# One vision-transformer layer on one core: the orders of all five engines written out, PSUM and exponential tiles in turn

## The chip, the core and the metric

The kernel runs on one core of one Trainium2 chip. The time is device microseconds of one execution. The core's engines each have their own instruction queue and run it in order: TensorE (PE: matrix products, with weight loads PEld), VectorE (DVE), ScalarE (ACT: functions such as sine and exponential), GpSimd (POOL), and SyncE (SP), which here issues nearly all DMA transfers. Engines wait for each other by semaphores. SBUF is the on-chip memory, PSUM the small memory into which TensorE writes.

## What is computed

Sixteen images of 3 x 512 x 512 are cut into 1024 patches of 768 values each and pass through one layer of width 256:

```python
h = patches @ W.T + b                                  # 16 x 1024 x 256
# attention, 8 heads of 32
q, k, v = split(layernorm(h) @ w_qkv)
k = sum_f kan_a[f]*sin(f*k) + kan_b[f]*cos(f*k)        # f = 1 .. 256, elementwise
attn = softmax(q @ k.T / sqrt(32))
h = h + (attn @ v) @ w_out + b_out
# feed forward: a shared network and the best 2 of 4 experts
x = layernorm(h)
h = h + shared(x) + sum over 2 experts of weight * expert(x)
```

All is in float32.

## The kernel before, in words

The 256 sines and cosines of every key element are made from sums of two angles: "slow" waves `w` and "fast" waves `f`. The keys' angles lie in DRAM (`ud`). For a *group* of eight rows of keys, DMA brings two tiles `w` of 128 x 1024 from `ud` (line 995), with each row repeated over many partitions; a third tile `f` is spread by a VectorE shuffle (line 1035, letter D below) from a source tile `src` that serves eight groups (line 1014). GpSimd multiplies each tile by its frequencies (L1050, T). ScalarE takes the sine (L1060, F). TensorE mixes the two `w` into a PSUM tile `kan` (L1080, M), VectorE multiplies that by `f` (L1094, P), TensorE adds up two such products (L1113, R). After eight groups the keys of one pair of heads are ready; VectorE splits them in a high and a low part (K) and they go through DRAM into their place.

Attention takes one pair of heads and half of the queries at a time. For each of eight key blocks, TensorE writes a score tile `sT` (L1179, S), ScalarE its exponential `es` (L1194, also F), TensorE adds it, weighed by values and by ones, into `av` (L1212, W). VectorE divides (N).

A *round* is four groups of waves (twelve sines) and eight scores and exponentials. ScalarE first does a round's exponentials and then the sines of another; a table load stands at each change (at L1332, behind the sines, a dummy exponential `few` forces it). An image has eight rounds.

All else is in four *chains*: generators that yield, step by step, on which engine their next step runs. Chain 0 makes keys, queries and values; chain 1 the output projection and the networks; chain 2 the experts' weights; chain 3 the tokens and the first layernorm. In an order a chain's step stands as the digit of the chain. Two steps matter below. `transposed_layernorm` lets GpSimd find the scale, ScalarE normalize four blocks `hn` (L546), TensorE transpose them in two groups `lnT` (L334) and ScalarE copy each into `hT` (L555). `gates` then multiplies `hT` by the gate weights (`gate`, L816): its first four products need the first copy, its last four the second.

Scores and `kan` share two PSUM buffers of 1024 columns, pool `big`: a score or a `kan` waits until the exponential or the product two tiles before it is done. Chain steps use two other PSUM buffers, `side`. The waves `w` have eight buffers, the `f` four, the exponentials five. TensorE works in three tilings: whole (scores, transposes), four columns of 32 (`av`, `red`, the gate) and eight tiles of 64 x 32 (`kan`); a chain step can be done whole (line 325) or in columns (line 328), and `tiling_of` picks the one that suits its neighbours.

The program is straight-line code, and Python lays it out: a planner holds a modelled clock for every engine. TensorE's order is a string, `ORDER`: for each token the planner lays that step on TensorE. Before it, `others` lays whatever on the other four engines can begin by then, the earliest first. So the other engines' orders, and SyncE's DMA issues, come from the planner's costs and due times. `begin` gives a step's earliest time from what it depends on; `put` queues the steps; `lay` and `lay_at` emit one. The eleven middle images repeat one piece of the string.

Of the kernel before, what the change touches and what calls it, by code (L numbers as in the profile page):

```python
# [11 lines left out]
FP = mybir.dt.float32  # L12
# [55 lines left out]
ORDER = (  # L68
    "33333331311003033003000M0M00M0M0MRR330M",
    "33R3M3MRM330M3R3MM0SRSSWSWSSWSSWWW0MWM3",  # L70
    "WRMMSSSRSSWWSSWSW0WWWM3MWMMRSSRSSWSWSSWSWWWW0WMMM0MRSSRSSWSSWSWSWWWWWMM0MMRSSSWSWSSWSSWW"
    "WRMWMWMRMSSSWSSWSWSSWRWWWW0M0M0MM0SSSRSSRWWWS3SW3SWWWW3MM31RMM1SSRWSWSSWSWSSWWWW3MM3MS10"
    "SRSWMWSSWW3SWSSR31WWW0MMMRMS0SS1WSS1WSW1R1SSWWW01MMWW1RM10SS1SMWSS1SSW1SWW1R01MMWWWWR1MM"
    "1SSR1SSW1SSWWSS1W1MMWWWMWMRS0S1SR1SSW1WW1SS1SWW01WWMM1WRM3SS1SSWWM1SSW1SS3R1WWWW1MWMM31S"
    "SRWM0SS1SS0SSWW0W3RW1WM01MM1SSWRWSS1SMW3SSWWR3SWWW1WWMM3RMM1SS0SSWWSS1SSW13WWRMM3WWWM31S"
    "SR1SSWMW1W1SS3RW3SS1WWWW10M1MM1RMS1SS0SSWWSSW1SRW01WWMM1SWW0RM10SS1SM1WR1SSWWSS1WW1WWWMM"
    "3SSRMMWS1SW1SS0SSWW0W1R3WMMWWM31SS1SSWRMW1WSS1SSW1WRW1WW10",
    (
        "MM1MM1RSS10SS1SSW1WW1SSW0RWWWWMM1RMM3SS0SSWWWSS1SS3RWW1WWW3MM10MM3SRRWSS1SSWS1SSWW3WWWMM"
        "3W31S1RM1MWS13SSR3SS1SSWW0WWW1WMMW1RMM1S0SS1SSW1SS0SWWWR1WWWW01MM10MM1SSR1WSSRWW1SS0SS1W"  # L80
        "WWWWMM1S0SRWSSWWMMW1SS3SS1WWWR13WMM31MM1RSS1SSWWWSS1SSRWWW1WW101"
    )
    * 11,
    "MM1MMR0SS1SS0SSWWW1SSW1RW3W1MM10MM1SSWW",
    "RSS1SS3RWW3SSWWW1WWW3MM1MMRS0SS1SSWS1SSWWRWWWWW3M31MM3SS1RM1SWWSSR1W3SSW3SW01WWWM1M0M1RM"
    "S1SS1SSWRWSSW1S01WWW1MM1WW0MM1SSR1SSWR1SSWWSS1WW0WWMMW1SS0SRSSWMWWS1SW1SMWWR10W1MMW1MM1R"
    "SS1SSW1SS1SSWWWRW1W1WW10MM10MM1SSR1SSWWSSW1SSRWW1MMWWWRMM1SS0SSWWSSWSSRWWW1MWW10M1RSS1SS"
    "WSSWSMWSMWWWWRMM1W1R1M1M1SS1SSWWSS1SSWW1RW1WW1WM1M1MS1RS1SSW1SSW1SSWMWWWRWMM1SWS1SRSSWMM"
    "WS1SW1SRW1WW1M1MW1WR1MS1SSWSWSS1SSWWWM1WR1MMWW1RM1M1SSRWSSW1SSWW1SSWWWWSS1SSWWSSWWSSWWWW"
    "S1SW1SS1SSWWSSWWWWW11110110111101000101010100010001000100",  # L90
# [3 lines left out]
def plain_path(ctx: ExitStack, tc: tile.TileContext, a: dict, out: bass.AP, verdict: bass.AP):  # L94
# [29 lines left out]
    esp = pool("esp", NES)  # L124
# [4 lines left out]
    big = pool("big", 2, PSUM)  # L129
# [151 lines left out]
    lanes = [0.0] * 8  # L281

# [142 lines left out]
    def lay(engine, queue):  # L425
        cost, deps, key, action = queues[engine][queue].pop(0)
        at = begin(engine, deps)
        clock[engine] = at + cost
        done[key] = clock[engine] + TAIL[engine]
        action()  # L430

    def heads(engine):
        for rank, (name, steps) in enumerate(queues[engine].items()):
            at = begin(engine, steps[0][1]) if steps else None
            if at is not None:
                yield at, rank, name

    def others(limit):

        soonest = None  # L440
        again = True
        while again:
            again = False
            soonest = None
            for engine in (SP, POOL, ACT, DVE):
                while True:
                    settle()
                    best = min(heads(engine), default=None)
                    chain = min(wanting(engine), default=None)
                    if chain and (  # L450
                        best is None
                        or chain[0] < best[0]
                        or (chain[0] == best[0] and best[2] not in ("prod", "keys"))
                    ):
                        at, lay_it = chain[0], lambda c=chain[1]: step(c)
                    elif best:
                        at, lay_it = best[0], lambda q=best[2]: lay(engine, q)
                    else:
                        break
                    if at > limit:  # L460
                        soonest = at if soonest is None else min(at, soonest)
                        break
                    lay_it()
                    again = True
        return soonest

    def lay_fixed(kind):

        cost, deps, key, action = queues[PE][kind][0]
        at = begin(PE, deps + (bigs[-2:-1] if kind in USERS else []))  # L470
        return at, lambda: lay_at(kind, at)

    def lay_at(kind, at):

        cost, deps, key, action = queues[PE][kind].pop(0)
        if kind == "S" and now["tiling"] is not None:
            cost += RELOAD
        clock[PE] = at + cost + retile(TILINGS.get(KINDS[kind]), at > clock[PE] + 0.03)
        done[key] = clock[PE] + TAIL[PE]
        user = USERS.get(kind)  # L480
        if user:
            bigs.append((user, *key[1:]))
        action()

    def run():

        order = "".join(ORDER)
        for i, token in enumerate(order):
            now["ahead"] = order[i + 1 : i + 4]
            while True:  # L490
# [1596 lines left out]
```

## Time and profile before

| what | value |
|---|---|
| runs shown | 3893.35, 3896.15, 3896.16 us; median 3896.15 |
| profiled execution, its run | 3898.54 us |
| profiled execution, its span | 3896.9 us |
| granted TensorE clock, mean | 0.994 |
| moved by DMA | 916.54 MB, 235 GB/s |
| sines (L1060), waves `w` and `f` | 1024 and 512, mean 1048 and 1046 ns |
| exponentials (L1194) | 1024, mean 1023 ns |
| GpSimd turns (L1050) | 1536, mean 1895 ns |
| shuffles (L1035) | 512, mean 1371 ns |
| products (L1094) | 512, mean 1215 ns |
| table loads | 128 at L1060, 128 at L1332, mean 1283 ns |

The profile is of one execution. "Busy" is the time in which an engine had an instruction in work; TensorE's ends are modelled and its instructions overlap, so its starts say more than its ends. A time line gives the start, the length, the engine, the line, the operation, its tiles as out<-in, the count, and in brackets the idle time before it with what ended that. Several instructions of a kind can stand in one row.

### The profile page before, as it was taken

The numbers are of one execution on the slowest core, as the hardware profiler recorded it, in microseconds if no ns is written. First come the engines' busy times: TensorE is split into PE (matmuls) and PEld (weight loads), VectorE is DVE, ScalarE is ACT, GpSimd is POOL, SyncE is SP. The second block draws the span as 40 slices with busy tenths as digits, with TensorE's granted clock in tenths as the row PEclk, the third lists the DMA queues.
The fourth block names the chain that finished last, engine by engine and source line by source line (L and its number), as shares of the span: only waits on it lengthen the run. The fifth ranks groups of instructions, "written<-read, shape, count | busy, mean of one in ns | idle before, by whom it ended". The sixth has DMA issues, their size and how long they took to land.

```text
span 3896.9 us, 103136 instructions
## 1 busy us (share of the span) xinstructions
PE 3791.3 (97%) x40457; PEld 1942.1 (50%) x40457; DVE 2544.1 (65%) x4075; ACT 3256.0 (84%) x3939; POOL 3193.6 (82%) x2328
## 2 busy tenths in 40 slices
PE   7899999999999999999999999999999999999998
PEld 4334454555545555455454545545455554544444
DVE  4657757666675766757666675776767667576652
ACT  2698888888888888888888888888888888889983
POOL 3899878888888878879788888878879888898860
PEclk9999999999999999999999999999999999999999
DMA  7898978878887887878888788788878888878760
GB/s 229 259 276 231 274 213 239 257 230 250 229 260 223 248 257 227 264 218 259 245 239 251 217 251 243 232 250 243 256 215 253 250 234 258 226 236 250 219 177 18
DMA packets 589665, 916.54 MB, mean 235 GB/s; under 512 B 60876, under 2 KB 179572, under 8 KB 589172
## 3 DMA queue, kind: packets, MB, share of 16 engines
q1 hardware_dynamic: 588036, 909.40, 79.6%
q8 instruction: 322, 5.28, 0.6%
q14 instruction: 171, 1.40, 0.1%
q10 hardware_dynamic: 1136, 0.47, 0.0%
HBM read 758.64 MB, written 150.99 MB: 233 GB/s over the span
## 4 chain that ended last, share of the span: by engine, by line
PE 77%; ACT 10%; DMA 7%; DVE 2%; issue 2%; POOL 1%; SPq 1%; ACTq 0%; POOLq 0%; DVEq 0%
PE av L1212 19%; PE sT L1179 11%; PE kan L1080 9%; PE red L1113 5%; PE tok L325 4%; ACT w L1060 4%; DMA w<-ud 3%; PE e1p L325 3%; PE tok L328 3%; PE e3p L325 3%; PE e1p L328 2%; ACT f L1060 2%; PE k L325 2%; PE proj L325 2%; PE s1p L325 1%
## 5 line engine op out<-in xcount | busy, mean ns | idle before, releaser
L1050 POOL TENSOR_TENSOR w<-w,lane 128x1024 int32<-128x1024 int32 x1024 | 1924.4, 1895 | 356.9 <-DMA w<-ud 252.2
L1194 ACT ACTIVATE es<-sT 128x1024 f32<-128x1024 f32 x1024 | 1004.0, 1023 | 369.0 <-PE sT L1179 305.9
L1060 ACT ACTIVATE w<-w 128x1024 f32<-128x1024 int32 x1024 | 1013.3, 1048 | 48.8 <-POOL w L1050 40.6
L1050 POOL TENSOR_TENSOR f<-f,lane 128x1024 int32<-128x1024 int32 x512 | 970.4, 1895 | 101.0 <-DVE f L1035 96.7
L1094 DVE TENSOR_TENSOR f<-kan,f 128x1024 f32<-128x1024 f32 x512 | 605.5, 1215 | 228.9 <-ACT f L1060 120.2
L1179 PE MATMUL sT<-q,k 128*128 128x512 f32 x2048 | 689.1, 450 | 14.0 <-DVE f L1094 7.8
L1035 DVE STREAM_SHUFFLE f<-src 128x1024 int32<-128x1024 int32 x512 | 681.1, 1371 | 1.0
L1212 PE MATMUL av<-es,v 128*32 128x256 f32 x8192 | 638.1, 383 | 11.1 <-ACT es L1194 11.1
L1212 PE MATMUL av<-es,ones 128*32 128x256 f32 x8192 | 630.5, 379 | 0.0
L1080 PE MATMUL kan<-w,coef 64*32 64x512 f32 x8192 | 529.3, 598 | 15.3 <-ACT w L1060 9.6
L1060 ACT ACTIVATE f<-f 128x1024 f32<-128x1024 int32 x512 | 514.2, 1046 | 13.1 <-POOL f L1050 13.1
L1179 PEld LDWEIGHTS sT<-q,k 128*128 128x128 f32 x2048 | 360.7, 189 | 254.0 <-issue 110.7
L1212 PEld LDWEIGHTS av<-es,v 128*32 128x32 f32 x8192 | 233.1, 109 | 347.9 <-issue 219.4
L1212 PEld LDWEIGHTS av<-es,ones 128*32 128x32 f32 x8192 | 266.5, 110 | 176.4 <-issue 0.9
L1236 DVE RECIPROCAL rc<-av 128x256 f32<-128x256 f32 x128 | 224.7, 1756 | 161.7 <-PE av L1212 161.6
L1080 PEld LDWEIGHTS kan<-w,coef 64*32 64x32 f32 x8192 | 123.9, 105 | 311.4 <-issue 144.7
L1113 PE MATMUL red<-f,pack 128*32 128x512 f32 x2048 | 269.8, 599 | 1.6 <-DVE f L1094 1.6
L325 PE MATMUL tok<-wt,x 128*128 128x256 f32 x780 | 186.9, 391 | 14.8 <-DMA x<-in_xT 11.2
L325 PEld LDWEIGHTS tok<-wt,x 128*128 128x128 f32 x780 | 147.4, 194 | 70.5 <-issue 29.2
L1060 ACT ACT_TABLE_LOAD x128 | 164.2, 1283 | 21.9 <-DMA w<-ud 19.7
L328 PE MATMUL tok<-wt,x 128*32 128x256 f32 x3024 | 176.3, 381 | 2.5 <-DVE ui L637 2.0
L1332 ACT ACT_TABLE_LOAD x128 | 164.2, 1283 | 2.2
(150 smaller groups left out, 4252.1 us busy)
## 6 DMA issues: line engine op xcount, KB each, us to landing
w<-ud SPq DMA_DIRECT2D x2048, 256.0 KB
q<-qd SPq DMA_DIRECT2D x512, 128.0 KB
k<-kd SPq DMA_DIRECT2D x256, 256.0 KB
x<-in_xT SPq DMA_DIRECT2D x128, 384.0 KB
ud<-u SPq DMA_DIRECT2D x64, 512.0 KB
ud<-ui SPq DMA_DIRECT2D x64, 512.0 KB
src<-ud SPq DMA_DIRECT2D x512, 64.0 KB
qd<-qhi SPq DMA_DIRECT2D x64, 256.0 KB
```

What stands on the lines that cost most here:

```text
L325: nc.tensor.matmul(out=out, lhsT=lhsT, rhs=rhs, start=start, stop=stop)
L328: nc.tensor.matmul(out=out[ts(i, 32)], lhsT=lhsT[:, ts(i, 32)], rhs=rhs, start=start, stop=stop)
L1035: nc.vector.stream_shuffle(w, sources[g // 8].rearrange("p r n -> p (r n)"), [4 * (g % 8) + i // 8 for i in range(32)],)
L1050: nc.gpsimd.tensor_tensor(w, w, f.to_broadcast([P, N]), ALU.mult)
L1060: nc.scalar.activation(x, w, AF.Sin, scale=TURN * 2.0**-32)
L1080: nc.tensor.matmul(out=ps[ds(64 * j + 32 * blk, 32), ts(r, 512)], lhsT=coef[ts(r, 64)].rearrange("p e f j -> p (e f j)"), rhs=w[ts(r, 64), ...
L1094: nc.vector.tensor_mul(w, kan.pop(g), w)
L1113: nc.tensor.matmul(out=rows_of_pair[p][ts(2 * i + r, 32), :], lhsT=pack[:, ds(PACK0 - 16 * (k % 2) - 2 * (k // 2), 32)], rhs=prod[:, ts(r, ...
L1179: nc.tensor.matmul(out=ps[:, ts(s, 512)], lhsT=k4[kc // 4][:, s, ts(kc % 4, P)], rhs=q4[:, s, :], start=True, stop=True,)
L1194: nc.scalar.activation(es, scores.pop(kc), AF.Exp, scale=SCALE)
L1212: nc.tensor.matmul(out=acc[0][ts(i, HD), ts(half, 256)], lhsT=ones32 if half else v[:, kc, p % NPAIR, ts(i % 2, HD)], rhs=es[:, ds(512 * ( ...
L1236: nc.vector.reciprocal(rc[0], acc[0][:, 256:512])
```

## The change

Instead of one order for TensorE there are five, one for each engine, all written out (`ORDERS`: a list of parts, each with its number of repeats and the orders of TensorE, ScalarE, VectorE, GpSimd and SyncE). The four loops that chose the other engines' steps are gone. `run` now looks at the next token of each engine, takes the one that can begin first by the planner's clock, and emits it; what is decided is only how the five fixed orders are woven into one program. A chain step that ends in a DMA says so (`SENDS`), and is emitted only when SyncE's order has come to the same chain's digit.

```diff
-ORDER = (
...
-        "MM1MM1RSS10SS1SSW1WW1SSW0RWWWWMM1RMM3SS0SSWWWSS1SS3RWW1WWW3MM10MM3SRRWSS1SSWS1SSWW3WWWMM"
-        "3W31S1RM1MWS13SSR3SS1SSWW0WWW1WMMW1RMM1S0SS1SSW1SS0SWWWR1WWWW01MM10MM1SSR1WSSRWW1SS0SS1W"
-        "WWWWMM1S0SRWSSWWMMW1SS3SS1WWWR13WMM31MM1RSS1SSWWWSS1SSRWWW1WW101"
-    )
-    * 11,
...
+STEPS = {
+    PE: {"M": "M", "R": "R", "S": "S", "W": "W"},
+    ACT: {"F": "fixed"},
+    DVE: {"P": "prod", "K": "keys", "N": "norm", "D": "spread"},
+    POOL: {"T": "turn"},
+    SP: {"A": "source", "W": "waves", "X": "tokens", "K": "keys", "Q": "queries"},
+}
+SENDS, SENT_KEYS = "sends", "S"
+ORDERS = (
...
+    (
+        11,
+        "MM1MMR1RSS10SS1SSW1WW1SSW0WWWWMM1RMM3SS0SSWWRSS1SS3WWWWWW1MM310MM1SSRRSS1SSWWSSW3W3WMMWW"
+        "3W31SSR1SSW1MMW1S3SWR3SSWW10W1WMMW1RMM1S0S1SSWWR1SS0SSWW1WWWW10MM10MM1SSRWSS1WWR1SS0SS1W"
+        "WWWWMM1SSR0WSSWMMWW1SS31SSWRWWW13MM13MMR1SS1SSWWSS1SSWRW1WWWW101",
+        "F1FFF1FF10FFFF1F1F0FFFFFF0FFFFFFFFFFF0FFFF3333F3FFFFFFFF3FFFFFFFFFFFFFFFFFFF1F1F1FF1FFFF"
+        "1FF1FF331332F3F3FF2FF1FFFFF1FFFF1FFF1FF1FFF1FFF1FFFFF1FFFFFFFF1FF1FFFFFFFFFFFFFFFFFFFFFF"
+        "1111F1F1FFFFF1FFFFFFFFFF12FFF1FFF12FFF1FFFFF1F",
+        "PPPP1DDDD1NNPP1PNPND3D3333KDD1N1PNNPN10PP010D1DD11131DP3P3NN3N333N3DPP1D2DKD000P2PN2NPPN"
+        "N0D00DD0D00NN0P1PNPPND0D1DKD10NPNNP1N111D1D0PP3DDNNNN3P1PP3PD22DD2KNNDNN",
+        "TTTTTTTTTTTTTTTTT3TTTTTT0TTT3T0TTTTT1TTTTTTT3TTTT22TTTTT20TT2T3T0TTTTT0TTTTTTTTTTTTTTTTT"
+        "T1TTTTTTTTTTTTTT22T2TTTT2TT",
+        "WWWWWWAWAWAWWWAWWWXQWSQ1WKWKWWW0WWWXAWAWWAAWWWWQWWSQKWKWWWX0WW0WAWA0WXWWAA0WWW0QWSW0KWWW"
+        "1KWWXWWWQ0AAWWAWAXQWXWWXWSWKQK",
+    ),
...
-    def others(limit):
...
     def run():
 
-        order = "".join(ORDER)
-        for i, token in enumerate(order):
...
+        settle()
+        while True:
+            heads = [(head(e), i) for i, e in enumerate(clock)]
+            heads = [(at, i) for at, i in heads if at is not None]
+            if not heads:
+                break
+            at, i = min(heads)
+            lay(list(clock)[i], at)
+            settle()
```

In SyncE's orders a W is one tile of waves (two transfers), an A one quarter of a source tile (two transfers of 64 KB), X a block of patches, K and Q the keys and queries of an attention, S the transfer of finished keys, a digit a chain's. Before, the four A of a source tile stood side by side in SyncE's queue; now there are W between them.

The two PSUM buffers of `big` and the five of the exponentials, which the pool handed out, are now named one by one:

```diff
-    esp = pool("esp", NES)
+    esp = pool("esp", 1)
...
-    big = pool("big", 2, PSUM)
+    big = pool("big", 1, PSUM)
...
-            ps = kan[g] = big.tile([P, N], FP, tag="big", name="kan")
+            ps = kan[g] = big.tile([P, N], FP, tag=f"big{len(bigs) % 2}", name="kan")
...
-            es = exps[kc] = esp.tile([P, 1024], FP, tag="es", name="es")
+            es = exps[kc] = esp.tile([P, 1024], FP, tag=f"es{(att * NT + kc) % NES}", name="es")
```

The instructions of ScalarE, VectorE, GpSimd and SyncE are the same in kind and number in both programs. On TensorE some chain steps take the other of their two forms (token products in columns: 1728 instead of 1512, whole: 336 instead of 390, and smaller differences of this kind), with the same work.

## The prediction

> **What bounds the kernel now.** I read the page's engine totals first, then its stretches (busy time of each engine between given times), then the time line around the places where TensorE's records leave room. The totals and the long middle stretch:
>
> ```profile
> span 3896.9 us, 103136 instructions
> PE 3791.3 (97%) x40457; PEld 1942.1 (50%) x40457; DVE 2544.1 (65%) x4075; ACT 3256.0 (84%) x3939; POOL 3193.6 (82%) x2328
> ...
> 0.00:100.00 100.00, 70.39 (x312) 44.98 (x312) 42.09 (x80) 25.31 (x38) 40.59 (x50) 0.93 0.74 231
> 100.00:400.00 300.00, 274.95 (x3035) 116.59 (x3036) 198.43 (x298) 250.01 (x287) 273.39 (x168) 0.97 0.89 257
> ...
> 700.00:3500.00 2800.00, 2769.47 (x30159) 1448.14 (x30161) 1882.54 (x3023) 2416.03 (x2931) 2373.37 (x1718) 1.00 0.83 241
> ```
>
> The columns of a stretch are its length, then busy time (and count) of TensorE, its weight loads, VectorE, ScalarE, GpSimd, then granted clock, DMA share, GB/s. From 0.7 to 3.5 ms TensorE is busy 2769 of 2800 us at clock 1.00: it is the bound there. From 0.1 to 0.4 ms GpSimd is at 91% and ScalarE at 83%: there they feed TensorE too slowly.
>
> "Busy" overstates TensorE, since matmul ends are modelled. So I took starts: records that follow each other undisturbed start 216 ns apart (256 columns), 429 ns (512), 230 ns (scores, 512 columns in one pass), with 93 to 136 ns more where the tiling (whole, four columns of 32, eight of 64x32) changes. All instructions of the program at these rates make 3519 us, its 1297 tiling changes 145 us. First instruction at 11 us and about 10 us after the last start: some 212 us are TensorE's waits. By place, in us: 90 before 400 us, 22 from 3600 us to the end of the matmuls, 86 in the 2800 us of the middle, of which half is a fixed surcharge (score pairs after another tiling, 0.11 each). What is left to win in the middle is about 43 us.
>
> The largest part of it returns once per image, at a matmul group `kan` behind the gate matmuls:
>
> ```profile
> 1567.54 1.28 ACT L1332 ACT_TABLE_LOAD   x1
> ...
> 1568.67 0.42 PE L816 MATMUL gate<-hT,gw 128*32 128x128 f32 x8
> 1568.83 0.20 ACT L1332 ACTIVATE few<-few 128x1 f32<-128x1 f32 x1
> 1568.94 0.57 ACT L555 COPY hT<-lnT 128x512 f32<-128x512 f32 x1
> ...
> 1569.41 1.03 ACT L1194 ACTIVATE es<-sT 128x1024 f32<-128x1024 f32 x1
> ...
> 1569.56 0.43 PE L816 MATMUL gate<-hT,gw 128*32 128x128 f32 x8 [0.47 <-ACT hT L555]
> ...
> 1570.49 1.09 PE L1080 MATMUL kan<-w,coef 64*32 64x512 f32 x16 [0.50 <-ACT es L1194]
> ```
>
> Gate work is 0.44 us and its tiling change 0.11, so `kan` should start at 1568.67 + 0.55 = 1569.22; it starts at 1570.49, 1.27 late. ScalarE is the cause: copy and first exponential of the round stand behind the table switch. Worked out alike at its eleven returns from 864 to 3220 us this is 1.27 us five times and 1.96 to 2.03 six times, 18.4 us together. I call it stall A. Stall B also returns once per image, where the first `av` of a round waits for the round's first exponential, 1.22 us:
>
> ```profile
> 1418.88 1.28 ACT L1332 ACT_TABLE_LOAD   x1
> ...
> 1420.28 1.92 ACT L1194 ACTIVATE es<-sT 128x1024 f32<-128x1024 f32 x2
> ...
> 1421.34 0.64 PE L1212 MATMUL av<-es,v 128*32 128x256 f32 x8 [1.01 <-ACT es L1194]
> ```
>
> **Buffers.** Followed by address through both programs, the 1536 `big` tiles already alternate between two PSUM places, with one exception, and the 1024 exponentials take their five buffers in turn without one. Naming the buffers removes no wait: at most that one exception, under 1 us. I take 0.
>
> **Stall A in the new order.** No instruction is added or removed on ScalarE, VectorE, GpSimd or SyncE; some TensorE steps change between whole and four-column form at equal work. Before, from the eighth score S8 of a round TensorE does six `av` (0.86 each), three token blocks (2.59), two `kan` (0.86), a transpose group (0.44), a score (0.46), a transpose group, `red` (0.86), `kan`, and 0.8 of tiling changes: the gate starts 18.5 us after S8. ScalarE ends exponential 8 about 1.4 after S8 (0.37 from a score's end to its exponential, 1.03 for itself), then does a table load (1.28), twelve sines at 0.95, four `hn` (0.52), a copy (0.57), table load and dummy (1.48), the second copy (0.57), the first exponential (1.03): it ends 19.8 after S8. The `kan` behind the gate needs that exponential's PSUM buffer and could run at 19.05: late by 0.85 with the 0.1 of the release, where the trace has 1.27 to 2.0. So such a count is good to about half a microsecond.
>
> After, TensorE does a fourth token block there, then transposes, two scores, `red`, transposes, two scores, one `av`, and only then the gate: third score at 20.6, gate at 22.4, first and second `kan` behind it at 23.0 and 23.8. ScalarE's first copy goes behind the table switch, the second behind two exponentials: first exponential ends at 1.4 + 17.8 = 19.2, second 20.2, copy 20.7, third 22.4 (its score ends at 21.0), fourth 23.4. Third score, gate and both `kan` have 1.3, 1.7, 0.5 and 0.4 us in hand. Stall A goes; the least cover is 0.4 us. If ScalarE comes later than that, it returns at the excess. Eleven images: -18.4 us, bounds -18.4 and 0.
>
> I made the same count for the other seven rounds of an image. Stall B stays: 15.2 us of ScalarE against 15.6 of TensorE, both unchanged. In the remaining six the first `av` and third score have 1.2 us or more, before and after. So 0 for these, bounds +1 and -1 us an image (the rest of the middle's 43 us, less 18 of A and 13 of B, is 12), +11 and -11.
>
> A rule that speaks against this: the Trainium skill (ScalarE: Activation LUTs, "What ACT_TABLE_LOAD costs") gives a switch of table sets about 1.28 us of load and 1.38 us of drain. The trace agrees with the load, 1.28, and shows no drain: the dummy starts at 1568.83, at the end of the load. With the drain, an estimate by that page, both switches of a round would be 2.8 us longer, the first exponential would end at 22.0, the third score would wait 1.4 us and A would come back in this form: the sum would lose most of its 18. I go by the trace.
>
> **Tiling changes.** Counted in both orders: 1297 before, 1260 after, 4.6 us less at 93 to 136 ns each. 28 of the 37 fall on the first three images (-3.3 us), where GpSimd and ScalarE set the pace; ten are one per image in the middle (-1.3). The first lie partly beside waits: I take -1.0 (bounds 0 and -3.3). The last images gain and lose: 0.
>
> **Start.** Source loads (`src`) leave SyncE from 65.1 us, behind the third `ud` pair, which waits for VectorE; the first fast shuffle starts at 74.1, GpSimd's first fast turn at 75.5, and from there GpSimd is busy to 99.7. In the new order two of the four parts go ahead of that pair: about 1.5 us earlier. `kan` may start one query block sooner, but queues behind the same turns. I take -0.7 (bounds 0 and -1.5).
>
> **SyncE, GpSimd, VectorE.** The first part of each source load moves 0.91 wave loads forward, mean of 64 loads, one wave load a 1.84 us slot (29.4 us a round over 16); the last part moves 2.4 back. It waits for a shuffle whose place among VectorE's products is unchanged. Its waits now, and those behind it (wave loads, then GpSimd's turns, then sines):
>
> ```profile
> SPq L1014 <- DVE f L1035: 129.9, 48, 4.9
> ...
> POOL w L1050 <- DMA w<-ud: 252.2, 104, 6.8
> ...
> ACT w L1060 <- POOL w L1050: 40.6, 32, 9.2
> ```
>
> The columns: total wait in us, times, longest. If all 64 wait 0.91 x 1.84 longer, SyncE loses 107 us; GpSimd's 252 us of waits reach ScalarE as 41, a sixth. That would be at most 18 us, beside ScalarE's 16% of idle time. I take 0, bounds 0 and +18.
>
> **Sum.** -18.4 - 1.3 - 1.0 - 0.7 = -21.4 us. The profiled span of 3896.9 becomes 3875.5, its run 3898.5 (1.6 around the span) 3877.1. The runs shown have the median 3896.15, 2.4 under the profiled run: 3874.8, said as 3875.
>
> **Rivals.** *The wait comes back* in the same round: the new cover is 0.4 us where my count missed the old stall by 0.4 to 1.2. For it: both sides of A are ScalarE's order, and ScalarE has only moved its copies. Against it: four checks all come out with cover. It leaves the tiling and the start, -3.0: 3893.
>
> *Slower: the source loads block SyncE.* One part at the head of the queue holds the wave loads behind it. It turns the result when more than (21.4 + 7.8) of the 107 us, 27%, reach TensorE; at half it is 3896.15 - 21.4 + 53.5 = 3928. For it: 48 of 64 loads wait there already, and go forward while their shuffle doesn't. Against it: a sixth is what passes on today, and the wave loads run up to eight buffers ahead.
>
> *The order on the chip isn't what its words say*: excluded for the buffers (they already alternate), and for the rest the two programs do differ; it would be 3896.
>
> **How the numbers follow.** This kernel's runs can tell 0.2%, 7.8 us, from no change. Forecast, faster by about 21: 0.66. Wait comes back or no effect: 0.14, nearly all within 0.2%. SyncE blocks, slower: 0.20. The range goes down to 3860 (3874.8 less 2.3 and 0.8 to the bounds of tiling and start and 11 in the other rounds) and up to 3906, half-way into the slower case.
>
> **What would show it.** Right: `kan` behind the gate starts within 0.6 us of the gate in the middle images; images return every 233.7 instead of 235.5 us (from 864.6 to 3219.6 in ten steps); `av` still waits 1.2 us once per image; clock 1.00. Wrong: a third score or `kan` in that round with an idle time ended by an exponential or copy; the wait of L1014 (its new line) on the shuffle above 200 us together with ScalarE waiting over 60 us for GpSimd. Gains of more than 5 us in the first 400 us would show that I undervalued the start.

## The result, and the profile after

The changed kernel takes 3894.49 us in the median (3888.84 to 3904.53, 12 runs) beside 3896.32 of the kernel before. The ratio is 0.9994, 95% interval 0.9983 to 1.0005: no change that can be told, where 21 us of gain were forecast. (In all that follows a ratio is that of a kernel to the kernel before, measured side by side; 0.001 is 3.9 us, and an interval is about 0.001 to either side.) The profiled execution of the changed kernel has a span of 3889.6 us; its own run took 3891.19.

Behind the orders' code the lines of the new program have numbers higher by 59, those of TensorE's chain steps (L325, L328, L334) by 83: L1050, L1060, L1080, L1094, L1113, L1179, L1194, L1212, L816, L546, L555, L1014 of before are L1109, L1119, L1139, L1153, L1172, L1238, L1253, L1271, L875, L605, L614, L1073 now. (The runs below have longer order texts and other line numbers again; go by the tiles.) Totals and the stretches that were shown of before:

```profile
span 3889.6 us, 104231 instructions
PE 3789.0 (97%) x41057; PEld 1937.2 (50%) x41057; DVE 2530.3 (65%) x4075; ACT 3261.8 (84%) x3939; POOL 3199.8 (82%) x2328
...
0.00:100.00 100.00, 66.85 (x282) 43.13 (x283) 39.35 (x76) 20.56 (x26) 38.34 (x49) 0.88 0.69 212
100.00:400.00 300.00, 276.47 (x3041) 125.76 (x3044) 203.14 (x307) 256.45 (x301) 276.95 (x170) 0.97 0.93 257
...
700.00:3500.00 2800.00, 2779.51 (x30979) 1442.12 (x30975) 1889.29 (x3038) 2435.74 (x2947) 2388.71 (x1724) 1.00 0.85 243
```

In the middle stretch all five engines are busy longer in the same 2800 us: TensorE's products 10 us, ScalarE 20 us. So the middle did become faster, and something at the ends was lost. The stretch of the round that the forecast was about:

```profile
1561.80 1.06 ACT L1119 ACTIVATE w<-w 128x1024 f32<-128x1024 int32 x1 [1.97 <-POOL w L1109]
...
1564.77 1.28 ACT L1391 ACT_TABLE_LOAD   x1
...
1566.17 0.57 ACT L614 COPY hT<-lnT 128x512 f32<-128x512 f32 x1
...
1566.64 1.94 ACT L1253 ACTIVATE es<-sT 128x1024 f32<-128x1024 f32 x2
...
1567.72 0.73 PE L1238 MATMUL sT<-q,k 128*128 128x512 f32 x2 [1.17 <-ACT es L1253]
...
1570.19 0.62 PE L875 MATMUL gate<-hT,gw 128*32 128x128 f32 x16
1570.74 1.95 PE L1139 MATMUL kan<-w,coef 64*32 64x512 f32 x32
```

Both `kan` follow the gate at once (1570.19 + 0.55 = 1570.74): stall A is gone. In this image the third score waits for the first exponential instead, and that comes late because ScalarE's sines had waited 1.97 us for a turn of GpSimd (1561.80). Counted as in the forecast, by what lies between the starts of TensorE's records beyond the undisturbed rate, over the ten middle images from 821 to 3180 us:

| TensorE waits, ten middle images | before | after |
|---|---|---|
| `kan` behind the gate (stall A) | 17.1 | 0 |
| first `av` of a round (stall B) | 12.2 (ten) | 6.1 (eight) |
| `red` behind the transposes | 4.1 | 0 |
| third score of A's round | 0 | 2.1 (two) |
| first score behind `e3p` (last layer of the networks) | 0 | 8.8 (seven) |
| all, with the fixed surcharges | 76.0 | 58.7 |

Images return every 233.7 us where it was 235.6 (last `av` of ten images: 821.1 to 3176.9 before, 824.2 to 3161.0 after). In the same count the waits from 400 to 800 us went from 11.9 to 20.3 us, and those from 3400 us on from 28.0 to 38.2. That is where the gain went.

This pair of executions shows more than the new middle is worth, though. Counted from the end of the 24th attention round to that of the 104th (VectorE's reciprocals `rc`), images return every 234.8 to 235.6 us, 235.2 in the mean, in the nine traces of this case with the old middle, and every 233.5 to 234.7 us, 234.0 in the mean, in the nine with the new one (e8 and e14 below mix the two and are left out). That is 1.2 us an image and not 1.9, or 13.5 us in eleven images.

### The profile page after: what moved, and what is told of

Same layout as the page of the kernel before. It is cut to its first block, busy times and chain, and to the rows that moved or that the text cites. A ratio compares the mean times of both kernels' runs of the same rounds, so it can differ in the third digit from the quotient of the medians.

```text
span 3889.6 us, 104231 instructions
## 1 busy us (share of the span) xinstructions
PE 3789.0 (97%) x41057; PEld 1937.2 (50%) x41057; DVE 2530.3 (65%) x4075; ACT 3261.8 (84%) x3939; POOL 3199.8 (82%) x2328
## 3 DMA queue, kind: packets, MB, share of 16 engines
q14 instruction: 169, 1.38, 0.1%
## 4 chain that ended last, share of the span: by engine, by line
PE 79%; DMA 7%; ACT 6%; DVE 3%; issue 2%; POOL 2%; SPq 1%; ACTq 0%; POOLq 0%; DVEq 0%
PE av L1271 20%; PE sT L1238 11%; PE kan L1139 10%; PE red L1172 5%; DMA w<-ud 4%; PE tok L411 4%; PE tok L408 4%; PE e3p L408 3%; PE e1p L408 3%; PE e1p L411 2%; ACT w L1119 2%; PE proj L408 2%; PE k L408 2%; PE s1p L411 2%; PE lnT L417 1%
## 5 line engine op out<-in xcount | busy, mean ns | idle before, releaser
L1109 POOL TENSOR_TENSOR w<-w,lane 128x1024 int32<-128x1024 int32 x1024 | 1928.2, 1898 | 296.4 <-DMA w<-ud 186.4
L1253 ACT ACTIVATE es<-sT 128x1024 f32<-128x1024 f32 x1024 | 1014.1, 1024 | 339.2 <-PE sT L1238 309.2
L1109 POOL TENSOR_TENSOR f<-f,lane 128x1024 int32<-128x1024 int32 x512 | 972.0, 1898 | 152.0 <-DVE f L1094 89.5
L1119 ACT ACTIVATE w<-w 128x1024 f32<-128x1024 int32 x1024 | 1016.1, 1048 | 58.8 <-POOL w L1109 47.7
L1153 DVE TENSOR_TENSOR f<-kan,f 128x1024 f32<-128x1024 f32 x512 | 613.3, 1218 | 291.5 <-PE kan L1139 135.3
L1238 PE MATMUL sT<-q,k 128*128 128x512 f32 x2048 | 677.2, 446 | 21.4 <-ACT es L1253 7.4
L1094 DVE STREAM_SHUFFLE f<-src 128x1024 int32<-128x1024 int32 x512 | 686.4, 1369 | 0.7
L1271 PE MATMUL av<-es,v 128*32 128x256 f32 x8192 | 638.9, 384 | 5.9 <-ACT es L1253 5.5
L1271 PE MATMUL av<-es,ones 128*32 128x256 f32 x8192 | 630.0, 379 | 0.0
L1139 PE MATMUL kan<-w,coef 64*32 64x512 f32 x8192 | 525.3, 597 | 8.3 <-ACT w L1119 6.9
L1119 ACT ACTIVATE f<-f 128x1024 f32<-128x1024 int32 x512 | 514.9, 1046 | 4.6 <-POOL f L1109 4.6
L1238 PEld LDWEIGHTS sT<-q,k 128*128 128x128 f32 x2048 | 359.0, 189 | 258.0 <-issue 104.5
L1271 PEld LDWEIGHTS av<-es,v 128*32 128x32 f32 x8192 | 228.4, 109 | 348.9 <-issue 225.4
L1271 PEld LDWEIGHTS av<-es,ones 128*32 128x32 f32 x8192 | 266.4, 110 | 176.1 <-issue 0.5
L1139 PEld LDWEIGHTS kan<-w,coef 64*32 64x32 f32 x8192 | 129.9, 105 | 295.9 <-issue 129.3
L1172 PE MATMUL red<-f,pack 128*32 128x512 f32 x2048 | 272.7, 602 | 3.2 <-DVE f L1153 3.1
L411 PE MATMUL tok<-wt,x 128*32 128x256 f32 x3456 | 199.8, 379 | 3.2 <-DVE h L643 3.2
L1119 ACT ACT_TABLE_LOAD x128 | 164.2, 1283 | 21.9 <-DMA w<-ud 19.7
L408 PE MATMUL tok<-wt,x 128*128 128x256 f32 x672 | 161.4, 393 | 14.9 <-DMA x<-in_xT 11.2
L605 ACT ACTIVATE hn<-h,less,rstd 128x256 f32<-128x256 f32 x256 | 138.2, 595 | 21.6 <-POOL less L597 21.1
```

What stands on the lines that cost most here:

```text
L408: nc.tensor.matmul(out=out, lhsT=lhsT, rhs=rhs, start=start, stop=stop)
L411: nc.tensor.matmul(out=out[ts(i, 32)], lhsT=lhsT[:, ts(i, 32)], rhs=rhs, start=start, stop=stop)
L1094: nc.vector.stream_shuffle(w, sources[g // 8].rearrange("p r n -> p (r n)"), [4 * (g % 8) + i // 8 for i in range(32)],)
L1109: nc.gpsimd.tensor_tensor(w, w, f.to_broadcast([P, N]), ALU.mult)
L1119: nc.scalar.activation(x, w, AF.Sin, scale=TURN * 2.0**-32)
L1139: nc.tensor.matmul(out=ps[ds(64 * j + 32 * blk, 32), ts(r, 512)], lhsT=coef[ts(r, 64)].rearrange("p e f j -> p (e f j)"), rhs=w[ts(r, 64), ...
```

## The experiments

**Which part of the new orders gains, which loses.** The five orders were cut at two places where each engine has done the same steps by both orders: behind the first three images and ahead of the last two. Each kernel has all orders written out and buffers named; only the letters differ.

```diff
 ORDERS = (start, middle * 11, tail)   # of all five engines
-new start, new middle, new tail
+e1_literal: old, old, old      e2_middle: old, new, old
+e3_start:   new, old, old      e4_tail:   old, old, new
```

> The orders that the kernel before ended up with on all five engines, written out as five literal orders, with the buffers named: the form of the change without its new orders. On ScalarE, VectorE, GpSimd and TensorE the sequence of instructions is that of before; on SyncE 32 entries among the first loads of weights change places with token loads. Theory 'ends' (the new orders win about 20 us in the middle images and lose most of it again in the first three and the last two): 3896 +-3, ratio 0.9995 to 1.0005. Rival 'form' (naming buffers and writing out orders costs something by itself, which eats the gain of the middle): 10 us or more above before.

Measured: 1.0005 (0.9996 to 1.0014). The literal form and the named buffers cost and bring nothing that can be told.

> Orders of before for the first three images and for the last two, new orders for the eleven images between. Theory 'ends': images return every 233.7 us instead of 235.5, and nothing is given back at the ends: 3896 - 1.9 x 10.5 = 3876, ratio about 0.995. Rival 'noise' (the split by stretches is the scatter of two executions, and the new middle is worth nothing in the median): 3894, ratio 0.9985 to 1.0. Rival 'elastic' (the last images wait for GpSimd and DMA anyway, so that TensorE's earlier arrival there is lost whatever the order of the last two images): about 3886, with the last two images longer by about 7 us than in before.

Measured: 0.9968 (0.9956 to 0.9979), 3883.31 us: some 12.5 us of gain, better than both kernels. The 0.995 of 'ends' lies outside the interval. The 3886 us of 'elastic' are nearer, but its sign isn't there: from the end of the 104th round the rest takes 718.5 us, before 719.6. Images return every 234.7 us in this trace. So part of the forecast gain is missing in the middle itself.

> New orders for the first three images alone, all else as before. Theory 'ends': the start is 3 to 5 us longer (the last av of the 24th round ended 3.1 us later in the profile of the changed kernel): 3900, ratio 1.0005 to 1.0015. Rival 'noise': 3896, ratio 0.9995 to 1.0005. My prediction on record (tilings and source loads at the start) would have it 1.7 us faster.

Measured: 1.0017 (1.0008 to 1.0026), some 6.6 us of loss.

> New orders for the last two images alone, all else as before. Theory 'ends': 6 to 9 us slower than before, since rounds 104 to 128 took 657.6 us instead of 650.8 and the rest behind them 1.8 us more: 3904, ratio 1.0015 to 1.0025. Rival 'elastic': the last images are no longer by themselves when they are reached no earlier: 3896, ratio 0.9995 to 1.0005.

Measured: 1.0016 (1.0007 to 1.0025), some 6.2 us of loss. The three add up to -12.5 + 6.6 + 6.2 = 0.3 us, which is the result within its interval. Against e1, which has their form, the start costs 0.0012 and the tail 0.0011. So the question is what the two ends lose.

**The compares beside GpSimd.** (The compares are the step of `gates`, L803, in which VectorE finds the order of the experts.) The longest new stalls of TensorE in the changed kernel are at 653 us (4.5 us) and 3461 us (4.7 us). The time line at the first:

```profile
644.91 5.43 DVE L803 TENSOR_TENSOR over<-gp 128x12 f32<-128x12 f32 x3
650.26 1.74 DVE L1295 RECIPROCAL rc<-av 128x256 f32<-128x256 f32 x1
651.93 2.28 DVE L1153 TENSOR_TENSOR f<-kan,f 128x1024 f32<-128x1024 f32 x2
...
653.14 2.20 PE L1172 MATMUL red<-f,pack 128*32 128x512 f32 x6 [2.69 <-DVE f L1153]
```

And GpSimd's in the same microseconds:

```profile
644.71 1.91 POOL L1109 TENSOR_TENSOR f<-f,lane 128x1024 int32<-128x1024 int32 x1
646.56 3.76 POOL L1109 TENSOR_TENSOR w<-w,lane 128x1024 int32<-128x1024 int32 x2
```

Three compares of 12 to 4 columns take 5.43 us, and the last ends at 644.91 + 5.43 = 650.34, where the third of GpSimd's turns ends (646.56 + 3.76 = 650.32): each compare lasts as long as a turn. The products wait behind them in VectorE's queue, and TensorE's `red` waits for the products. At 3451 us three compares take 5.43 us again. There the steps that make the angles of the next keys stand behind them, and TensorE's `e1p` waits for the last of these:

```profile
3450.95 5.43 DVE L803 TENSOR_TENSOR over<-gp 128x12 f32<-128x12 f32 x3
...
3460.76 2.69 PE L408 MATMUL e1p<-hT,w1e 128*128 128x512 f32 x4 [2.84 <-DVE ui L696]
```

In the kernel before three compares took 0.3 to 2.0 us in all gates but two (3.6 at most). The Trainium skill (SBUF — State Buffer, "SBUF: two separate sides") has VectorE and GpSimd share a pair of ports under an exclusive lock, held for a whole instruction; a VectorE instruction with two SBUF operands needs it against a GpSimd instruction that reads SBUF. The run takes one operand to PSUM:

```diff
 # first gate step, gate logits ps in PSUM
+lg = small("gwt"); nc.vector.tensor_copy(lg, ps)
+for d in range(1, NE):
+    tensor_tensor(over[d], lg[0 : NE - d], ps[d:NE], ALU.is_ge)
 # second gate step, softmax p in SBUF
-for d in range(1, NE):
-    tensor_tensor(over[d], p[0 : NE - d], p[d:NE], ALU.is_ge)
```

> The changed kernel, but VectorE's three compares of the gate (which find the order of the experts) read the logits, one operand in PSUM and one in a small SBUF copy made just before (one more instruction of about 0.17 us a gate), instead of the two softmax operands in SBUF; the exponential keeps the order of the experts, so the result is the same. Theory 'shared port' (VectorE instructions with two SBUF operands are held up while GpSimd runs a turn of 1.9 us; instructions that read PSUM are not): the three compares take about 0.5 us in every one of the 32 gates instead of 0.3 to 5.4, the stalls of TensorE at about 653 us (4.5 us) and 3461 us (4.7 us) shrink below 1 us each, and the time falls from 3894.5 by 6 to 9 us, to 3885 to 3888. Theory 'order of the step' (the gate step stands in front of the products, whatever its length): the stalls shrink by less than half, and the time falls by 0 to 3 us.

Measured: 0.9971 (0.9959 to 0.9983), 3882.49 us. The rows of the compares, of the changed kernel and then of this run (count, shortest, median and longest in ns, first and last start):

```profile
L803 DVE TENSOR_TENSOR over<-gp x96: 153/178/1929, 414.8 to 3848.1; 128x12 f32<-128x12 f32 x32, 128x8 f32<-128x8 f32 x32, 128x4 f32<-128x4 f32 x32
```

```profile
L796 DVE TENSOR_TENSOR over<-gwt,gateT x96: 153/156/170, 405.4 to 3835.3; 128x12 f32<-128x12 f32 x32, 128x8 f32<-128x8 f32 x32, 128x4 f32<-128x4 f32 x32
```

With an operand in PSUM none of 96 takes over 170 ns, and the stalls at 653 and 3461 us are gone: the products begin at 648.45 where it was 651.93, and `red` follows without a wait. The edit also moves the compares forward in VectorE's queue, so that GpSimd's turns beside them have to be looked at: in this run 87 of the 96 compares begin inside a turn (more than 0.06 us before its end), and still none is long. In the changed kernel none of the 70 short compares begins so, and each of the 26 that took 1.70 us or more ends 0.02 to 0.03 us behind the end of a turn. So it is the operand, which agrees with the lock that the page describes; the step's place alone doesn't explain it.

> Control: the orders of before written out (ratio 1.0005 in the run e1) with the compares on the logits. Theory 'what was lost in the new orders came from the compares at two places': in the orders of before no compare stands in front of a stall (they took 2.0 us in most gates, 3.6 at most), so the ratio is 0.9995 to 1.0005, and the gain in e5 (0.0023) belongs to the new orders. Theory 'a gain anywhere': VectorE's shorter gate step is worth the same with any order, ratio 0.998.

Measured: 0.9998 (0.9989 to 1.0007). In the old orders the same edit brings 0.0007 against e1, within the intervals; in the new ones 0.0023. So 0.0016 of that belong to the new orders.

> The new orders for the last two images alone (ratio 1.0016 in the run e4) with the compares on the logits. Theory 'shared port': the stall at about 3465 us (4.5 us) goes, ratio 1.0016 less 0.0012, 1.0002 to 1.0006, the rest being the stalls at 3530, 3615, 3636 and after 3840 us. Theory 'other stalls make the loss': 1.0013 or more.

Measured: 1.0000 (0.9991 to 1.0009). The whole loss of the tail goes with the compares: 0.0016 by these ratios, and against the controls with all old orders 0.0011 (e4 and e1) becomes 0.0002 (e11 and e10).

**The start, first try: a gate step behind a wait.** At 404 us the new VectorE order has the keys' split K, which waits 3.6 us for a transfer, ahead of a gate step; ScalarE's exponential of the gate, which stands ahead of an exponential and the sines, idles 4.5 us.

```diff
 VectorE, about 400 us:
-DDK1002PPD0
+DD1K002PPD0    e6_gate_first
+DD12KPP00D0    e9_gate_early (and e12, e13, e16, e17), with the compares of e5
```

> The changed kernel with one exchange in VectorE's order: at about 404 us the first step of a gate (row maximum and difference) goes ahead of the splitting of finished keys K, where it stood behind it. Theory 'K blocks the gate' (K waits 3.6 us for the transfer that holds its buffers, the gate's exponential waits behind it for VectorE, and ScalarE stands 4.5 us with four sines and an exponential behind it): ScalarE's idle time at 401 to 406 us goes, the stalls of TensorE at 409 to 421 us (4.6 us) shrink below 1.5 us, and the time falls by 3 to 4.5 us, to about 3891. Theory 'elastic' (what is won here is waited for later, since GpSimd and the transfers set the pace of the start): the stalls there shrink but the time stays within 1 us of 3894.5.

Measured: 0.9984 (0.9974 to 0.9993), an improvement of 0.0010 on the changed kernel, within the intervals. ScalarE's wait went, but the next one in VectorE's queue took its place:

```profile
400.82 0.21 ACT L876 ACTIVATE gp<-gp 128x16 f32<-128x16 f32 x1 [0.23 <-DVE gp L874]
...
410.17 0.69 DVE L769 TENSOR_SCALAR u<-k 128x512 int32<-128x512 f32 x1 [4.55 <-DMA kd<-klo]
...
416.69 3.05 PE L1255 MATMUL red<-f,pack 128*32 128x512 f32 x8 [4.22 <-DVE f L1236]
```

The key step at 410 us waits for the transfer of the keys just split, and the products stand behind it.

> The run e5 (changed kernel, compares on the logits; ratio 0.9971), and in VectorE's order at about 404 us both gate steps go ahead of the keys K, and the two products P ahead of the two key steps that wait for transfers (from K, gate 1, keys, keys, gate 2, P, P, keys to gate 1, gate 2, K, P, P, keys, keys, keys). Theory 'waiting steps stand ahead of ready ones' (K waits 3.6 us and the key steps 3.9 us for transfers, and the products that TensorE needs stand behind both): the stalls of TensorE at 409 to 421 us, 3.7 us in e5, go below 1 us, and the ratio falls by 0.0007 to 0.0012 against e5, to about 0.9961. Theory 'elastic': the stalls move on and the ratio stays at 0.997.

Measured: 0.9974 (0.9962 to 0.9986), no better than e5. The stalls at 409 to 420 us are gone from this trace, the time isn't lower, and at 710 us TensorE waits 3.45 us, beside 2.49 in e5: "elastic" holds here.

> The new orders for the first three images alone (ratio 1.0017 in the run e3), with the compares on the logits and VectorE's gate steps and products at 404 us moved ahead as in e9. If the two places (404 to 421 and 645 to 660 us) are the loss of the start: 0.9995 to 1.0001 (4.0 and 3.9 us of stalls less, of 6.6 lost). If the loss is spread over the other places (570, 715 us): 1.0008 or more.

Measured: 1.0009 (0.9999 to 1.0020). By these ratios both places together are worth 0.0008 of the start's 0.0017, and about half stays. Against the controls the start costs 0.0012 without the two edits (e3 and e1) and 0.0011 with them (e12 and e10). Such a difference is good to about 0.0013 either way, so the times show no gain here; the trace shows that the two waits went and a third grew.

**The start, second try: keys that SyncE holds.** What is left in e12's trace against that of the control (e10) is one place, 700 to 840 us: TensorE waits 8.5 us there, 2.7 in the control. The time line of e12 (keys split on VectorE, sent and read back by SyncE, first score):

```profile
687.09 0.69 DVE L796 TENSOR_TENSOR klo<-red,khi 128x512 fp32r<-128x512 f32 x1
...
693.01 0.48 SPq L1276 DMA_DIRECT2D kd<-khi  x1
693.72 0.33 SPq L1276 DMA_DIRECT2D kd<-klo  x1
...
698.50 1.19 SPq L1287 DMA_DIRECT2D k<-kd  x2
...
702.22 1.51 SPq L1287 DMA_DIRECT2D k<-kd  x2
...
704.47 2.05 PE L1323 MATMUL sT<-q,k 128*128 128x512 f32 x4 [2.50 <-DVE rc L1380]
```

The keys are split by 687.8 and leave at 693.0. The releaser named at the score is the one with the last event; the transfers are what remains to be tested.

```diff
 TensorE, about 701 us:   (S S tokens S S queries S S)
-MMWWSS3SS0SSRWWMM
+MMWW3SS0SSSSRWWMM    e13_tokens_first (on e12)
 SyncE, about 685 to 704 us:
-QW0WSK1WKWX
+Q0SWWKK1WWX          e16_keys_sent (on e12), e17_repaired (on e9)
```

> The run e12 (new orders for the first three images, compares on the logits, gate ahead at 404 us; ratio 1.0009), with one exchange in TensorE's order at about 701 us: the token product and the query product of the chains go ahead of the scores that open the next pair of heads (from S S tokens S S queries S S to tokens S S queries S S S S). Theory 'keys late' (the first score waits 2.5 us for the keys' way through DRAM, split by VectorE at 691 us, read back by transfers that leave at 698.5 us, while 5 us of other work stands behind it): the stall at about 704 us goes and those at 705 and 709 us shrink, 2.5 to 3.5 us less, ratio 1.0000 to 1.0004. Theory 'elastic' (the first exponential behind the table load comes later by as much): the stalls move to the next scores and the ratio stays at 1.0008 to 1.0010.

Measured: 1.0019 (1.0010 to 1.0028). The first score no longer waits, the fifth does, for the second half of the same keys; here the releaser is named:

```profile
711.11 1.53 PE L1323 MATMUL sT<-q,k 128*128 128x512 f32 x4 [2.04 <-DMA k<-kd]
```

So the keys are late, and moving TensorE's work did not help.

> The run e12 (new orders for the first three images, compares on the logits, gate ahead at 404 us; ratio 1.0009), with SyncE's order changed at one place, about 685 to 704 us: the finished keys are sent right behind the queries' transfer and both halves are read back together (from Q W 0 W S K 1 W K W X to Q 0 S W W K K 1 W W X). In e12 VectorE had split the keys by 687.8 us, SyncE sent them at 693.0, since loads of waves that waited for buffers stood ahead, and the halves were read back from 698.5 and 702.2 us. Theory 'SyncE holds the keys': they are sent at about 689 us, read back from about 694, the score at 704 us no longer waits (2.5 us, and 2.3 us at the fifth score in e13), and the ratio falls to 0.9998 to 1.0002. Theory 'elastic': the waves held up behind the keys now make ScalarE wait, and the ratio stays at 1.0007 or more.

Measured: 1.0002 (0.9992 to 1.0011). Of its time line:

```profile
691.26 0.69 DVE L796 TENSOR_TENSOR klo<-red,khi 128x512 fp32r<-128x512 f32 x1
...
693.23 0.32 SPq L1276 DMA_DIRECT2D kd<-khi  x1
...
699.01 2.48 SPq L1287 DMA_DIRECT2D k<-kd  x4
...
706.77 1.19 PE L1323 MATMUL sT<-q,k 128*128 128x512 f32 x4
```

The keys leave 1.3 us after their split instead of 5.2, all four transfers are read back together, and the score at 706.8 us doesn't wait. (This execution stands 4 us later than that of e12 already at the end of its 16th round, 588.4 us to 584.7; the spacing is what counts.) From 700 to 840 us TensorE is now busy 139.11 us of 140, beside 137.04 in e12 and 139.93 in the control e10.

> The run e9 (all new orders, compares on the logits, gate ahead at 404 us; ratio 0.9974) with the same change of SyncE's order at about 690 us. Theory 'SyncE holds the keys': ratio 0.9960 to 0.9967, beside 0.9955 of the run e7, which has the new orders in the middle alone. Theory 'elastic': 0.9972 to 0.9975.

Measured: 0.9961 (0.9948 to 0.9974), 3882.32 us. The expected value is met. From 700 to 840 us TensorE is busy 139.15 us, beside 136.55 in e9. So the traces settle that SyncE held the keys, and that TensorE gets back 2.1 and 2.6 us there. The whole times show it only in direction: 0.0007 from e12 to e16 and 0.0013 from e9 to e17 are within the intervals.

**The middle.** Is its gain the one round of the gate? Old orders, and only that round new on some engines:

```diff
 each middle image, positions of the order:
+e8_a_alone:        TensorE 84-132, ScalarE 89-133 new
+e14_three_engines: the same, and VectorE 56-93 new
```

> The orders of before written out, and in the eleven middle images only the round of the gate changed, on TensorE (positions 84 to 132 of the 240 of an image) and ScalarE (positions 89 to 133 of 222), to the new orders; VectorE, GpSimd and SyncE as before. Theory 'A alone': the kan behind the gate no longer waits, the images return every 233.8 to 234.0 us, and most of the gain of the new middle (12.5 us) is here: 3884 to 3887. Theory 'all five engines': the two engines' new orders without the others' make a new wait in the same round, and less than half of the gain is left: 3890 or more. Theory 'elsewhere': the gain of the middle comes from the other seven rounds: 3892 or more, with the stall gone.

Measured: 1.0100 (1.0085 to 1.0116), a loss of 39 us. Stall A is gone from the trace and a longer one is there:

```profile
1588.79 0.22 ACT L876 ACTIVATE gp<-gp 128x16 f32<-128x16 f32 x1 [2.86 <-DVE gp L874]
```

In ScalarE's new order the gate's exponential comes earlier; VectorE's old order makes its operand behind two products (the second at 1587.25). ScalarE waits with the exponentials of scores behind it, and images take 239 us.

> The run e8 (orders of before, in the middle images the gate's round new on TensorE and ScalarE; ratio 1.010), with VectorE's new order for that round too (positions 56 to 93 of 160). Theory 'the orders belong together' (the 4 us an image lost in e8 came from ScalarE's exponential of the gate, which stood waiting 2.9 us for VectorE, whose gate step still stood behind two products): the wait goes, the images return every 233.6 to 234.2 us, and the ratio is 0.9950 to 0.9975, so that the gain of the new middle (0.9968) is in this one round. Theory 'GpSimd and SyncE too': a wait for waves or sources stays, ratio 0.998 to 1.005. Theory 'other cause': 1.008 or more.

Measured: 1.0372 (1.0354 to 1.0389), far on the side of the third theory by its number, but the trace shows the second theory's cause, a wait for waves:

```profile
1626.20 0.22 POOL L908 TENSOR_TENSOR gwt<-gwt,gs 128x16 f32<-128x16 f32 x1 [5.53 <-DVE gs L906]
...
1632.95 1.06 ACT L1202 ACTIVATE w<-w 128x1024 f32<-128x1024 int32 x1 [3.58 <-POOL w L1192]
...
1634.06 1.93 PE L1222 MATMUL kan<-w,coef 64*32 64x512 f32 x8 [3.58 <-ACT w L1202]
```

GpSimd's old order has a gate step ahead of its next turns, and VectorE's new order makes the operand `gs` of that step later. GpSimd waits 5.53 us here, 62.1 us in all beside 1.1 before; sines and `kan` wait behind it, and images take 247 us. Pieces of two solutions don't fit together, so whether stall A alone makes the middle's gain was not isolated; only the counts speak for it. In all nine traces with the new middle stall A is gone, and in all nine scores wait behind `e3p`, which they do in none with the old one.

**A version that beats both.** The new middle with the compares of e5, old start and tail:

> The kernel with the new orders in the eleven middle images alone (measured 3883.3), with the compares of the gate reading the logits as in the run e5. Theory 'shared port': here no compare is known to stand in front of a stall, so the gain is 0 to 4 us: 3879 to 3883. Theory 'order of the step': 3883 to 3884, one instruction more in each of 32 gates at no cost.

Measured: 0.9955 (0.9941 to 0.9970), 3879.18 us, the lowest ratio of all, though its interval overlaps with those of e2, e5, e17 and e18. Two more steps from there:

```diff
 e15_scale_gpsimd, second gate step:
-nc.vector.tensor_mul(p, p, s); nc.vector.tensor_reduce(m, p, max)
+nc.gpsimd.tensor_tensor(p, p, s, mult)      # m equals s
 e18_keys_middle, SyncE, once per middle image:
-0QWSW0KWWW1KWW
+0QSWW0KWWW1KWW
```

> The run e7 (new middle, compares on the logits; ratio 0.9955) with the last VectorE instruction of the gate that has two operands in SBUF taken away too: the product with the reciprocal of the sum goes to GpSimd (one more instruction of about 0.2 us there), and the maximum behind it is left out, since it equals that reciprocal. Theory 'shared port': 1.7 us less of VectorE in most of 32 gates, but no stall is known to hang on it now: ratio 0.9945 to 0.9956. If GpSimd, which works 82% of the span, is what the middle waits for: 0.9957 or more.

Measured: 0.9972 (0.9959 to 0.9984): no gain, rather a loss, on the side of "GpSimd is what the middle waits for"; but the intervals overlap, and this stays open.

> The run e7 (new orders in the middle images, compares on the logits; ratio 0.9955) with one exchange in SyncE's order of a middle image: finished keys are sent ahead of the load of waves that stood before them (from queries, queries read, W, keys sent, W to queries, queries read, keys sent, W, W). In e7 eight of ten images have a score that waits 0.7 to 2.5 us (14.0 us together) for the keys to be read back. Theory 'SyncE holds the keys': they leave some 1.5 to 2.4 us earlier, 8 to 12 of the 14 us go, ratio 0.9925 to 0.9938. Theory 'elastic': the waits go to the fifth score or to the waves, ratio 0.9950 to 0.9957.

Measured: 0.9962 (0.9949 to 0.9976): no gain. Of the changed kernel, and then of e18:

```profile
1177.56 1.19 SPq L1202 DMA_DIRECT2D k<-kd  x2
...
1183.53 1.17 PE L1238 MATMUL sT<-q,k 128*128 128x512 f32 x4 [1.90 <-DMA k<-kd]
```

```profile
1163.52 0.37 SPq L1276 DMA_DIRECT2D kd<-khi  x1
...
1168.83 1.24 SPq L1287 DMA_DIRECT2D k<-kd  x2
...
1178.68 2.05 PE L1323 MATMUL sT<-q,k 128*128 128x512 f32 x4 [3.02 <-DMA w<-ud]
```

In the changed kernel the score waits for keys that were asked for 6 us before. In e18 they are sent within 0.1 us of their split, yet the score waits, now put down to a load of waves. Over the ten images TensorE's waits went from 64.7 (e7) to 63.4 us. The middle's late keys are real, and this exchange doesn't win them.

## Why the prediction was wrong

*Buffers:* right. e1 gives 1.0005 for the two named pools and the written-out orders together.

*Stall A:* right in mechanism, and in size for this wait: 17.1 us in ten images to 0. The cover was overrated at one place: the third score, for which 1.3 us in hand were counted, waits 1.4 and 0.7 us in two images, because the count of ScalarE had no wait for GpSimd in it (1.97 and 1.27 us ahead of these two). That images return every 233.7 us as forecast is luck of this trace; 234.0 is the mean of nine, and 235.2 that of before.

*Stall B:* forecast unchanged at 1.2 us per image; it fell to 0.6 in the mean, and stands in eight images of ten. It was moved more than won: it is small where the score ahead of it waits behind `e3p`. At 1184 us that score waits 2.1 us and the `av` not at all, at 1415 us the score doesn't wait and the `av` 1.2 us.

*The other seven rounds, 0 within 11 us either way:* the waits of the scores behind `e3p`, 8.8 us in ten images, are new, and B and `red` gave 10.2 back. In this pair the sum is near 0 by cancelling. Over all the traces it isn't: of the 19.7 us counted for the middle (18.4 and 1.3) e2 shows some 12.5, and the nine traces of each kind 13.5; e7 shows 16.8 against its control (0.9955 and 0.9998), with a wider interval. So this term was some 6 to 7 us a loss, inside its bounds.

*The table-load rule:* the new round's load (1564.77) and the copy behind it (1566.17) are 1.40 us apart, of which 1.28 are the load: no drain of 1.38, as the trace before had it. The sine before the load ends at 1564.75, so none stands ahead of it either.

*The step that failed* is above all the one on the ends: "The last images gain and lose: 0", and for the start -0.7 and -1.0 for tiling changes. By themselves the tail cost 6.2 us and the start 6.6. That is 14.5 us off; the rest, some 7, is the middle. Two things were left out of the working. VectorE's gate step was never priced: its three compares cost 0.3 to 5.4 us according to GpSimd's turns, and in the new orders they met three turns at two places where TensorE's operands stand behind them. And of SyncE only the source loads were counted. For the tail this is shown (e11); for the start the traces show three waits, the times only a part. The rival on the source loads is refuted by its own sign:

```profile
SPq L1073 <- DVE f L1094: 107.7, 41, 10.3
```

The wait of the source loads fell from 129.9 us, and ScalarE's waits for GpSimd's waves are 47.7 us, under the 60 that were named. But the finished keys, which the term didn't look at, were held 5 us behind loads of waves. The new order also parts the two reads of the keys (K and W in turn in SyncE's string), which the prediction didn't take up: the two stand side by side for 60 of 64 pairs in the old order and for 5 in the new one.

*The range* held the time by luck: its upper end allowed for a loss by source loads that block SyncE, and the loss came from VectorE's compares, other transfers and the middle. The rival of a returning wait named 3893, near the 3894.49 measured, but that wait came back by only 2.1 us in ten images.

## What to carry to other kernels

When orders of all engines change, count the ends of the program as closely as its repeated middle: eleven images won what five others lost. Price a short instruction by the longest duration that its rows show, and see who stands behind it in its queue; if it has two SBUF operands and GpSimd is busy, take one from PSUM, as e5 does. An order found for all engines together is one solution: parts of it on some engines alone cost 39 and 145 us here. And one pair of traces is one draw: images came 1.9 us sooner in the first pair and 1.2 in the mean of nine.

## What the hardware showed that was not expected

VectorE's small compares with two SBUF operands last until GpSimd's running turn ends. Of the changed kernel's 96 compares 70 took 0.15 to 0.25 us and 26 took 1.70 to 1.93, none a time between; a mean tells nothing of them.

TensorE's clock falls to half for 3.4 us where it has just stood still. Stretches at 653 us of the changed kernel, columns as above:

```profile
649.00:653.00 4.00, 1.45 (x16) 0.24 (x8) 4.00 (x3) 3.29 (x5) 4.00 (x3) 0.96 0.98 239
652.70:656.10 3.40, 2.96 (x14) 1.06 (x18) 3.37 (x6) 1.34 (x2) 2.77 (x9) 0.50 1.02 251
656.10:659.50 3.40, 3.40 (x48) 0.88 (x40) 3.22 (x6) 1.45 (x2) 0.33 (x1) 1.00 1.04 229
```

TensorE works 1.45 of 4 us, runs at 0.50 for 3.4 us, and then at 1.00 again. Between 300 and 3800 us the traces of before, after and all runs but e8 and e14 show 41 such windows (two of them twice as long), and each stands at a wait of TensorE of 1.87 us or longer (two pauses right behind each other, as in stall A, counted as one). Not each such wait draws one: of the six waits of 2.0 us that stall A had in the trace before, one did (2041 us). So a wait of 2 us can cost up to 1.7 us more, an estimate (half of 3.4), and one of 1.3 us drew no window in these traces. The Trainium skill (TensorE: Matmul & The Clock Gate, "What's actually happening") has a free-running window of about 3.4 us, which agrees with the length and with the chance in it; it names an idle stretch of such a window as the condition, where here 1.87 us of wait was enough. Whether this makes part of the spread between runs (3888.84 to 3904.53 for the changed kernel) was not tested.
